# Four graph-attention layers on one core: fewer factor columns from one transfer, a front in halves with the activation table first, and a last output closed head by head

## The chip, the cores and the metric

The kernel runs on one core of one Trainium2 chip. The metric is the device time in microseconds. Before the change it is 3103.57 us, the median of three runs (3102.70 to 3105.31); the profiled execution took 3104.86 us and its profile spans 3103.1 us. The program holds two versions of the computation: a fast one, and a slow general one that is entered only if a flag says that the inputs leave the fast one's assumptions. In these runs only the fast one works.

Names used below: PE is the matrix engine (TensorE), DVE the vector engine, ACT the scalar engine with its activation tables, POOL is GpSimd, SP the engine that issues most transfers.

## What is computed

The input `x` is 16 batches of 1024 nodes with 256 features, `adj` is one 1024 x 1024 integer adjacency matrix. Four layers follow each other, each of them `x = x + layer(relu(layernorm(x)))`:

```python
# --- layer 0 (adj_preln) ---
h = jnp.maximum(_layernorm(x, axis=-1), 0.0)
x = x + _L0_gnn_ref(h, adj, L0_gnn_W, L0_gnn_a)
# layers 1, 2 and 3 in the same way, with _L1_, _L2_ and _L3_

# layer 0 (4 heads of 64 features; layers 1 and 3 differ in heads and mask only)
Wh = (h @ W).reshape(h.shape[0], h.shape[1], N_H, D_F)
a_src, a_dst = (a[:, :D_F], a[:, D_F:])
s_src = jnp.einsum('bnhd,hd->bnh', Wh, a_src)
s_dst = jnp.einsum('bnhd,hd->bnh', Wh, a_dst)
e = s_src[:, :, None, :] + s_dst[:, None, :, :]
e = jnp.where(e > 0, e, NEG_SLOPE * e)          # NEG_SLOPE = 0.2
e = jnp.where(mask, e, -jnp.inf)
alpha = jax.nn.softmax(e, axis=2)
h_out = jnp.einsum('bijh,bjhd->bihd', alpha, Wh)
return jax.nn.elu(h_out)
```

Layers 0 and 3 have four heads of 64 features, layer 1 has one head of 256. Layer 2 scores by a product of two projections of the nodes (512-wide products) instead of by two columns, and ends in a relu.

In layers 0, 1 and 3 the kernel needs no exponential for each pair of nodes. With `s_i` for the source and `s_j` for the other node, `exp(leaky(s_i + s_j))` is, up to a factor that only depends on `i` and falls out of the softmax, `exp(s_j) * max(exp(0.8 s_i), exp(-0.8 s_j))`. So three exponentials for each node and head are enough: `exp(s_j)` scales the values, `exp(0.8 s_i)` is spread as a row (`row`), and `exp(-0.8 s_j)` is a column (`ke`). The exponents come out of the projection itself: the weights `w` carry a few more columns, the products of `W` and `a`.

## The kernel before

A small scheduler (`Plan`) collects every step with its engine, an assumed cost and a due time, and lays all batches and layers into one order for each engine. The due times follow from constants:

```python
PERIOD, EARLY = 190.0, 0.39
START = {0: 0.0, 1: 0.9852, 2: 2.2118, 3: 3.5247}
LEAD = {0: 0.62, 1: 0.38, 2: 0.32, 3: 0.87}
STEP = {0: 0.0465, 1: 0.0464, 2: 0.0538, 3: 0.0718}
# WHEN, LATER and AHEAD: shifts for single layers and batches (left out)
```

Each engine runs its own list strictly in that order, so a step that waits holds up everything behind it on its engine.

The weights and their factor columns, three for each head. `first` is the weight of layer 0, whose columns DVE makes; for the others POOL multiplies and ACT adds up:

```python
t = const.tile([P, KC, F + 3 * heads], F32, name=name)
...
def load_a():
    tiles["a"] = buf("p1", [P, 2, heads, d], name="a_bc")
    for side in range(2):
        queue.dma_start(
            out=tiles["a"][:, side],
            in_=bass.AP(tensor=a.tensor, offset=a.offset + side * side_step,
                        ap=[[0, P], [head_step, heads], [1, d]]),
        )
...
for c in range(KC):
    for side, to in ((1, 0), (0, 2)):
        # columns: wa = W[c] * a[side]              (DVE or POOL, L666)
        # add_up:  sum over d into column(s), with
        scales = (1.0, SLOPE - 1.0) if side else (1.0 - SLOPE,)
```

The prologue of a layer: statistics of `x`, then the reciprocal deviation (DVE L833, POOL L836, DVE L839), the normed rows `h` on ACT (L870), their transposes on PE (L886), a copy to SBUF on ACT (L901), the projection on PE, and the eviction:

```python
cols = F + 3 * heads if self.gat else F
...
product(pv[:, :cols], T["hT", t0][:, c, k * P : (k + 1) * P], w[:, c, :cols], ...)
...
a = self.val[:, t, :, d : d + 1]
nc.scalar.activation(a, T["pv", t][:, F : F + heads].unsqueeze(2), AF.Exp)               # L931
nc.scalar.activation(self.ke[:, :, t], T["pv", t][:, F + heads : cols], AF.Exp)          # L932
```

`product` splits each stationary tile into two of 64 columns, and the profile shows two matmuls for each of these in float32. The first layer of the first batch has its statistics in one piece, ahead of the first `rstd`:

```python
due, step = SOON, 0.1
stats = [statistics(b, t, due - 1, (loads[b][t],)) for t in range(NT)]
```

The attention of the layers with four heads. `weigh` runs on DVE, `attend` on PE; each `p` tile of 128 x 512 feeds four products, which are 16 matmuls of 65 columns in the profile:

```python
nc.vector.scalar_tensor_tensor(          # L1063
    p, lay.rows[half, hd], lay.ke[:, hd, jt : jt + 1], mask_of(half, jt), op0=OP.max, op1=OP.mult)
...
product(T["acc", half, hd][:, t, :], p[:, t * P : (t + 1) * P], lay.val[:, jt, hd, :], ...)
```

When a head is summed, it is divided by its denominator; after the last head of a half of the nodes the elu, the residual and, in layer 3, the store are done for all heads together:

```python
if hd != heads - 1:
    continue
its = (half * HT, (half + 1) * HT)
s = lay.elu(T, half, its, at - early[0], (s,), (4, 2.3, 2.45), ("o",))
# elu: ACT exp (L1035), ACT relu(1 - exp) (L1036), DVE max (L1040), DVE add to x (L1041)
```

Of the kernel before, what the change touches and what calls it, by code (L numbers as in the profile page):

```python
# [44 lines left out]
PERIOD, EARLY = 190.0, 0.39  # L45
START = {0: 0.0, 1: 0.9852, 2: 2.2118, 3: 3.5247}
LEAD = {0: 0.62, 1: 0.38, 2: 0.32, 3: 0.87}
STEP = {0: 0.0465, 1: 0.0464, 2: 0.0538, 3: 0.0718}
WHEN = {
    (1, "weights"): ((-0.3018, 0.0087), (-0.0444, 0.0088)),  # L50
    (1, "attended"): ((0.2222, 0.0273), (0.109, 0.1164)),
    (2, "weights"): ((0.0221, 0.0304), (0.2823, 0.0096)),
    (2, "attended"): ((0.438, 0.0374), (0.6199, 0.0376)),
# [3 lines left out]
    (0, 3): 0.058, (1, 0): 0.06, (1, 1): 0.618, (2, 0): -0.057, (2, 1): -0.091, (3, 0): -0.332, (3, 1): -0.137,  # L57
    (3, 2): 0.022, (12, 2): 0.228, (12, 3): 0.316, (13, 1): 0.259, (13, 3): 0.414, (14, 1): -0.085,
    (14, 2): 0.134, (14, 3): -0.14, (15, 1): -0.188, (15, 2): 0.165, (15, 3): -0.487,
}  # L60
AHEAD = {
    (0, 3): -0.158, (1, 0): 0.374, (2, 0): 0.124, (2, 1): -0.123, (3, 2): -0.288, (15, 2): -0.045,
    (15, 3): -0.78,
# [7 lines left out]

# [460 lines left out]
def fast(  # L532
# [95 lines left out]
    def weight(w, name, due, a=None, heads=0, side_step=0, head_step=0):  # L628


        t = const.tile([P, KC, F + 3 * heads], F32, name=name)

        def load():
            queue.dma_start(out=t[:, :, :F], in_=w.rearrange("(c p) f -> p c f", p=P))

        queue = nc.scalar if name == "w0" else nc.sync
        engine = ACT if name == "w0" else SP
        s = landed(plan.add(engine, 0.5, due, load), due, 256)
        if a is None:
            return t, s  # L640
        d = F // heads
        tiles = {}

        def load_a():
            tiles["a"] = buf("p1", [P, 2, heads, d], name="a_bc")
            for side in range(2):
                queue.dma_start(
                    out=tiles["a"][:, side],
                    in_=bass.AP(
                        tensor=a.tensor,  # L650
                        offset=a.offset + side * side_step,
                        ap=[[0, P], [head_step, heads], [1, d]],
                    ),
                )

        s2 = landed(plan.add(engine, 1.2, due, load_a, take=("p1",)), due, 256)


        first = name == "w0"
        done = []  # L660
        for c in range(KC):
            for side, to in ((1, 0), (0, 2)):

                def columns(c=c, side=side, to=to):
                    wa = tiles["wa", c, side] = buf("u", [P, heads, d], name="wa")
                    (nc.vector if first else nc.gpsimd).tensor_mul(  # L666
                        wa, t[:, c, :F].rearrange("p (h d) -> p h d", h=heads), tiles["a"][:, side]
                    )

                def add_up(c=c, side=side, to=to):  # L670
                    wa, lo = tiles.pop(("wa", c, side)), F + to * heads
                    scales = (1.0, SLOPE - 1.0) if side else (1.0 - SLOPE,)
                    if first:
                        nc.vector.tensor_reduce(t[:, c, lo : lo + heads], wa, AX.X, OP.add)
                    for k, scale in reversed(list(enumerate(scales))):
                        to_all = t[:, c, lo + k * heads : lo + (k + 1) * heads]
                        if first:
                            if scale != 1.0:
                                nc.vector.tensor_scalar(to_all, t[:, c, lo : lo + heads], scale, None, op0=OP.mult)
                            continue  # L680
                        for hd in range(heads):
                            junk = small.tile([P, F], BF16, name="junk_a", bufs=1)[:, :d]
                            nc.scalar.activation(  # L683
                                junk, wa[:, hd, :], AF.Identity, scale=scale, accum_out=to_all[:, hd : hd + 1]
                            )

                last = c == KC - 1 and side == 0
                give = ("u", "p1") if last else ("u",)
                after = (s, s2, *done[-1:])
                m = plan.add(*((DVE, 0.4) if first else (POOL, 1.0)), due + 0.5, columns, after, take=("u",))  # L690
                cost = 0.65 if first else (1 + side) * (1.0 if heads > 1 else 0.4)
                done.append(plan.add(DVE if first else ACT, cost, due + 0.5, add_up, (m,), give=give))
        return t, done[-1]

    first_x = load_x(0, SOON)
    w0, w0_ready = weight(w_l0, "w0", SOON, a_l0, 4, F // 4, F // 2)
# [38 lines left out]
    w1, w1_ready = weight(w_l1, "w1", 20.0, a_l1, 1, F, 2 * F)  # L735
    w2v, w2v_ready = weight(w3_l2, "w2v", 30.0)
    w3, w3_ready = weight(w_l3, "w3", 50.0, a_l3, 4, F // 4, 0)
# [68 lines left out]
    class Layer:  # L806
# [7 lines left out]
        def prologue(self, due, step, stats, direct=False):  # L814
# [6 lines left out]
            cols = F + 3 * heads if self.gat else F  # L821
# [5 lines left out]
            for n, its in enumerate(parts):  # L827
# [26 lines left out]
                s = plan.add(DVE, 0.2, due, norm, (*stats[its], ready[-1] if n else None))  # L854
                s = plan.add(POOL, 2.0, due, norm2, (s,))
                take = () if n else (tag,) if self.gat else (tag, "hq")
                ready += [plan.add(DVE, 0.2, due, norm3, (s,), take=take)] * (its.stop - its.start)
# [35 lines left out]
            for n, t0 in enumerate(range(0, NT, 2)):  # L893
# [11 lines left out]
                for k in range(2):  # L905
# [18 lines left out]
                    def evict(t=t):  # L924
# [6 lines left out]
                        nc.scalar.activation(a, T["pv", t][:, F : F + heads].unsqueeze(2), AF.Exp)  # L931
                        nc.scalar.activation(self.ke[:, :, t], T["pv", t][:, F + heads : cols], AF.Exp)  # L932
# [41 lines left out]
            if direct:  # L974
                for half in range(2):
                    for hd in range(heads):

                        def spread(half=half, hd=hd):
                            pd = T["pd", half, hd] = buf("pp", [P, HALF])
                            for k in range(HT):  # L980
                                col = self.ke[:, heads + hd, half * HT + k : half * HT + k + 1]
# [14 lines left out]
            def factors():  # L996
                er = T["er"] = buf("pp", [P, P])
                nc.tensor.transpose(er[:n, :], self.ke[:, heads:, :].rearrange("p h t -> p (h t)"), ident)  # L998
# [29 lines left out]
        def elu(self, T, key, its, due, after, sizes, give):  # L1028

            tag = f"ex{sizes[0]}"  # L1030
            xs = lambda: x_tiles[self.b][:, its[0] : its[1], :]

            def up():
                T["ex", key] = buf(tag, [P, its[1] - its[0], F])
                nc.scalar.activation(T["ex", key], T["o", key], AF.Exp)  # L1035
                nc.scalar.activation(T["ex", key], T["ex", key], AF.Relu, bias=1.0, scale=-1.0)  # L1036

            def down():
                o, ex = T["o", key], T["ex", key]
# [3 lines left out]
            s = plan.add(ACT, sizes[1], due, up, after, take=(tag,))  # L1043
            s = plan.add(DVE, sizes[2], due, down, (s,), give=(tag, *give))
            for t in range(its[0], its[1]):
                self.finish(t, due, (s,))
# [5 lines left out]
    def steps_a(lay, due, span):  # L1052
# [4 lines left out]
        for i in range(n):  # L1057
# [56 lines left out]
            if hd != heads - 1:  # L1114
                continue
# [289 lines left out]
```

## Time and profile before, and how to read them

| what | value |
|---|---|
| median of three runs | 3103.57 us |
| span of the profile | 3103.1 us |
| PE busy | 3058.2 us |
| DVE busy | 2716.4 us |
| ACT busy | 1354.5 us |
| POOL busy | 128.3 us |
| DMA over the span | 123.22 MB, mean 40 GB/s |

The page of the profile first gives the busy time of each engine, then the busy share in 40 equal slices of the span (77.6 us each), the DMA queues, the chain of work that ended last, and the groups of instructions by line, with their count, busy time and mean length. A matmul's end is modelled and matmuls overlap in the pipeline, so the mean length of a single one is much longer than the distance from one to the next, and a PE that is shown busy need not be at its best rate. Besides the page, the trace answers for parts of the span: a timeline of instructions (start, length, engine, line, what is written and read, and in brackets the idle time before and what ended it), the busy time of each engine in windows, the chain of waits in order of time, and the same groups kept apart by shape.

### The profile page before, as it was taken

The numbers are of one execution on the slowest core, as the hardware profiler recorded it, in microseconds if no ns is written. First come the engines' busy times: TensorE is split into PE (matmuls) and PEld (weight loads), VectorE is DVE, ScalarE is ACT, GpSimd is POOL, SyncE is SP. The second block draws the span as 40 slices with busy tenths as digits, with TensorE's granted clock in tenths as the row PEclk, the third lists the DMA queues.
The fourth block names the chain that finished last, engine by engine and source line by source line (L and its number), as shares of the span: only waits on it lengthen the run. The fifth ranks groups of instructions, "written<-read, shape, count | busy, mean of one in ns | idle before, by whom it ended". The sixth has DMA issues, their size and how long they took to land.

```text
span 3103.1 us, 108725 instructions
## 1 busy us (share of the span) xinstructions
PE 3058.2 (99%) x48836; PEld 2160.0 (70%) x48836; DVE 2716.4 (88%) x5532; ACT 1354.5 (44%) x3369; POOL 128.3 (4%) x99
## 2 busy tenths in 40 slices
PE   7899999999999999999999999999999999999998
PEld 5776757777676776767767676676767767665766
DVE  7999868999989899898989989899899989787797
ACT  5454465443533445334443433434334453345343
POOL 1000000000000000000000000000000000000000
PEclk9999999999999999999999999999999999999999
DMA  3111002102011110101102011020111101000110
GB/s 127 33 54 33 19 29 73 46 30 60 22 40 46 36 46 23 60 23 36 46 26 60 23 36 47 26 60 22 43 43 33 53 30 39 19 22 29 33 36 24
DMA packets 83577, 123.22 MB, mean 40 GB/s; under 512 B 8544, under 2 KB 44192, under 8 KB 83104
## 3 DMA queue, kind: packets, MB, share of 16 engines
q1 hardware_dynamic: 81776, 115.66, 12.4%
q8 instruction: 385, 6.31, 0.8%
q14 instruction: 88, 0.72, 0.1%
q10 hardware_dynamic: 1328, 0.52, 0.1%
HBM read 98.83 MB, written 17.33 MB: 37 GB/s over the span
## 4 chain that ended last, share of the span: by engine, by line
PE 96%; DVE 2%; DMA 1%; ACT 0%; issue 0%; POOL 0%; SPq 0%; POOLq 0%; DVEq 0%
PE pp L574 32%; PE acc L574 31%; PE accb L574 29%; PE pp L886 4%; DVE p L1063 1%; DMA a_bc<-in_L_gnn_a_dram 1%; DMA raw<-in_adj_dram 0%; DVE bn L800 0%; PE pp L998 0%; DVE xt L1041 0%; PE pp L982 0%; DVE o L1040 0%; DVE mv L801 0%; ACT junk_a L683 0%; POOL rstd L836 0%
## 5 line engine op out<-in xcount | busy, mean ns | idle before, releaser
L1063 DVE SCALAR_TENSOR_TENSOR p<-row,ke,mask 128x512 f32<-128x512 f32 x2048 | 1424.5, 745 | 94.5 <-PE acc L574 91.7
L574 PEld LDWEIGHTS acc<-val,p 128*64 128x64 f32 x32768 | 1066.9, 138 | 202.0 <-issue 109.0
L574 PE MATMUL acc<-val,p 128*64 128x65 f32 x32768 | 1095.4, 223 | 12.1 <-DVE p L1063 11.1
L574 PE MATMUL accb<-val,p 128*64 128x257 f32 x8192 | 926.1, 380 | 0.0
L574 PEld LDWEIGHTS accb<-val,p 128*64 128x64 f32 x8192 | 569.7, 136 | 291.3 <-issue 9.5
L574 PE MATMUL pp<-qT,hT 128*64 128x512 f32 x2048 | 471.5, 593 | 0.0
L574 PE MATMUL pp<-w,hTp 128*64 128x268 f32 (+1 forms) x3072 | 376.3, 388 | 0.7 <-ACT hTp L901 0.7
L1169 ACT ACTIVATE u<-pp 128x512 f32<-128x512 f32 x256 | 152.4, 595 | 323.2 <-PE pp L574 229.4
L574 PEld LDWEIGHTS pp<-w,hTp 128*64 128x64 f32 x3072 | 209.6, 137 | 107.8 <-issue 6.2
L870 ACT ACTIVATE h<-xt,nshift,rstd 128x256 f32<-128x256 f32 x512 | 272.5, 595 | 17.0 <-DVE nshift L839 15.7
L574 PEld LDWEIGHTS pp<-qT,hT 128*64 128x64 f32 x2048 | 133.0, 137 | 190.4 <-issue 184.9
L1209 ACT ACTIVATE o<-accb,rdens 128x256 f32<-128x256 f32 x128 | 60.7, 474 | 424.8 <-DVE rdens L1201 384.9
L800 DVE BATCH_NORM_STATS2 bn<-xt 128x6 f32<-128x256 f32 x512 | 212.5, 415 | 13.6 <-DMA xt<-in_x_dram 4.3
L836 POOL TENSOR_TENSOR rstd<-rstd,neg_half 128x8 f32<-128x8 f32 (+1 forms) x66 | 119.6, 1813 | 2371.9 <-DVE rstd L833 2094.5
L1207 ACT ACTIVATE o<-accb,rden 128x256 f32<-128x256 f32 x128 | 60.7, 475 | 336.4 <-DVE rden L1201 335.5
L1175 DVE TENSOR_TENSOR p<-p,mask 128x512 f32<-128x512 f32 x256 | 177.1, 692 | 8.9
L1142 DVE SCALAR_TENSOR_TENSOR p<-row,ke,mask 128x512 f32<-128x512 f32 x256 | 181.1, 743 | 0.0
L1174 DVE SCALAR_TENSOR_TENSOR p<-u,p 128x512 f32<-128x512 f32 x256 | 174.5, 682 | 5.9 <-ACT p L1170 5.7
L1170 ACT ACTIVATE p<-pp,shift_col 128x512 f32<-128x512 f32 x256 | 174.9, 683 | 0.0
L931 ACT ACTIVATE val<-pp 128x4 f32<-128x4 f32 (+1 forms) x384 | 66.8, 174 | 202.3 <-PE pp L574 202.2
L1040 DVE SCALAR_TENSOR_TENSOR o<-ex,o 128x256 f32<-128x256 f32 (+1 forms) x192 | 131.8, 686 | 16.0 <-ACT ex L1036 16.0
L901 ACT COPY hTp<-pp 128x512 f32<-128x512 f32 x192 | 104.6, 588 | 88.7 <-PE pp L886 88.6
(82 smaller groups left out, 1849.8 us busy)
## 6 DMA issues: line engine op xcount, KB each, us to landing
row<-er_d SPq DMA_DIRECT2D x272, 256.0 KB, 3.2
xt<-in_x_dram SPq DMA_DIRECT2D x32, 512.0 KB, 5.1
out_dram<-xt SPq DMA_DIRECT2D x32, 512.0 KB, 3.1
raw<-in_adj_dram SPq DMA_DIRECT2D x4, 1024.0 KB
raw<-in_adj_dram SPq DMA_DIRECT2D x16, 256.0 KB, 3.2
w<-in_L_gnn_W_dram SPq DMA_DIRECT2D x2, 256.0 KB
a_bc<-in_L_gnn_a_dram SPq DMA_DIRECT2D x4, 128.0 KB, 10.3
wraw<-in_L_gnn_W_dram SPq DMA_DIRECT2D x2, 256.0 KB
```

The lines of the kernel that those rows point to most:

```text
L574: nc.tensor.matmul(to[c : c + COLS], stationary[:, c : c + COLS], moving, start=start, stop=stop, skip_group_check=True,)
L800: nc.vector.bn_stats(st, x_tiles[b][:, t, :])
L836: nc.gpsimd.tensor_tensor(T["rstd"][:, its], T["rstd"][:, its], neg_half[:, its], OP.pow)
L870: nc.scalar.activation(h, x_tiles[b][:, t, :], AF.Relu, bias=T["shift"][:, t : t + 1], scale=T["rstd"][:, t : t + 1],)
L886: nc.tensor.transpose(tp[:, c, k * P : (k + 1) * P], T["h", t0 + k][:, c * P : (c + 1) * P], ident)
L1040: nc.vector.scalar_tensor_tensor(o, ex, -1.0, o, op0=OP.mult, op1=OP.max)
L1063: nc.vector.scalar_tensor_tensor(p, lay.rows[half, hd], lay.ke[:, hd, jt : jt + 1], mask_of(half, jt), op0=OP.max, op1=OP.mult)
L1142: nc.vector.scalar_tensor_tensor(p, lay.rows[half, 0], lay.ke[:, 0, jt : jt + 1], mask_of(half, jt), op0=OP.max, op1=OP.mult)
L1169: nc.scalar.activation(u, e, AF.Exp, scale=1.0 - SLOPE)
L1170: nc.scalar.activation(p, e, AF.Exp, bias=shift_col, scale=SLOPE)
L1174: nc.vector.scalar_tensor_tensor(p, u, 1.0, p, op0=OP.max, op1=OP.mult)
L1175: nc.vector.tensor_mul(p, p, mask_of(half, jt))
```

## The change

The change has five parts.

1. **A factor column less for each head.** `exp(s_j)` is no longer read from a column of its own. The column `-0.8 s_j` is there already, and the activation's scale of `1 / (SLOPE - 1)` turns it back. The projection of layers 0 and 3 has 264 columns in place of 268, that of layer 1 has 258 in place of 259.
2. **`a` from one transfer.** Both sides of `a` come in one contiguous piece for each partition; the factors 0.8 and -0.8 are put on `a` itself by two DVE operations (L656 after the change) instead of on the sums. For layer 3, whose `a` is shared by the heads, only one copy is loaded.
3. **The front.** Statistics and `rstd` of the first half of the nodes are placed ahead of those of the second half, and a dummy exponential on ACT loads the activation table ahead of the first needed activation.
4. **The end.** In the last half of the last layer of the last batch, elu and residual are done head by head, the division of the last head moves from ACT to DVE, and the store is split into the first three heads and the last.
5. **New constants** for the scheduler, which change the order of the work on every engine.

```diff
-PERIOD, EARLY = 190.0, 0.39
-START = {0: 0.0, 1: 0.9852, 2: 2.2118, 3: 3.5247}
+PERIOD, EARLY = 190.0, 0.56
+START = {0: 0.0, 1: 0.9446, 2: 2.175, 3: 3.5153}
 ... (LEAD, STEP, WHEN, LATER and AHEAD in the same way)
-        t = const.tile([P, KC, F + 3 * heads], F32, name=name)
+        t = const.tile([P, KC, F + 2 * heads], F32, name=name)
 ...
-            for side in range(2):
-                queue.dma_start(
-                    out=tiles["a"][:, side],
-                    in_=bass.AP(... ap=[[0, P], [head_step, heads], [1, d]]),
+            queue.dma_start(
+                out=tiles["a"].rearrange("p h s d -> p (h s d)"),
+                in_=bass.AP(tensor=a.tensor, offset=a.offset, ap=[[0, P], [1, own * 2 * d]]),
+            )
+        def sign():
+            for side, by in enumerate((1.0 - SLOPE, SLOPE - 1.0)):
+                of = tiles["a"][:, :, side, :]
+                nc.vector.tensor_scalar(of, of, by, None, op0=OP.mult)
 ...
+    def warm():
+        nc.scalar.activation(faults[:, 0:1], ones, AF.Exp)
+    plan.add(ACT, 1.6, SOON, warm)
 ...
-            cols = F + 3 * heads if self.gat else F
+            cols = F + 2 * heads if self.gat else F
 ...
+                at = due - 2 * (direct and n == 0)
+                s = plan.add(DVE, 0.2, at, norm, (*stats[its], ready[-1] if n else None))
 ...
-            nc.scalar.activation(a, T["pv", t][:, F : F + heads].unsqueeze(2), AF.Exp)
-            nc.scalar.activation(self.ke[:, :, t], T["pv", t][:, F + heads : cols], AF.Exp)
+            nc.scalar.activation(
+                a, T["pv", t][:, F + heads : cols].unsqueeze(2), AF.Exp, scale=1.0 / (SLOPE - 1.0))
+            nc.scalar.activation(self.ke[:, :, t], T["pv", t][:, F:cols], AF.Exp)
 ...
+            ending = lay.b == B - 1 and lay.layer == 3 and half == 1
+            on_act = lay.filling and not (ending and hd == heads - 1)
 ...
-            if hd != heads - 1:
+            if ending:
+                cols, sizes = (hd * d, (hd + 1) * d), (4, 0.8, 0.8)
+            elif hd == heads - 1:
+                cols, sizes = (0, F), (4, 2.3, 2.45)
+            else:
                 continue
 ... (elu on these columns; the store after head 2 takes three heads, that after head 3 the last)
-            stats = [statistics(b, t, due - 1, (loads[b][t],)) for t in range(NT)]
+            stats = [statistics(b, t, due - (3 if t < HT else 1), (loads[b][t],)) for t in range(NT)]
```

## The prediction

> **What bounds the kernel now.** First the page: engine totals and slices.
>
> ```profile
> PE 3058.2 (99%) x48836; PEld 2160.0 (70%) x48836; DVE 2716.4 (88%) x5532; ACT 1354.5 (44%) x3369; POOL 128.3 (4%) x99
> ...
> PE   7899999999999999999999999999999999999998
> ```
>
> PE is busy nearly always; only the first and the last slices (77.6 us each) fall short. But a busy PE may still be stretched, so I ask at what distance matmuls follow each other at best. The chain of waits, in order of time, gives runs of one kind:
>
> ```profile
> 1136.62 6.07 PE acc L574 x208
> 1158.21 10.44 PE accb L574 x96
> 1198.04 6.87 PE pp L574 x32
> 1220.15 3.61 PE pp L574 x32
> 1346.52 10.44 PE accb L574 x96
> ```
>
> So 29.2 ns for 65 columns (6.07/208), 108.75 ns for 257, 214.7 ns for 512 and 113 ns for 268; a 128-wide transpose takes 127.5 ns (8 in 1.02 us, same view). The run of 96 `accb` comes back after 188.31 us: that is the steady state, one batch.
>
> Counts by shape (the groups kept apart by shape) times these distances: 32768 x 29.2 = 957 us, 8192 x 108.75 = 891, 2560 of 512 columns 550, 2048 of 268 columns 232, 1024 of 259 and 1024 of 256 about 223 (interpolated), 1142 transposes 146, masks and the rest 7. **Sum: 3004 us.** The span is 99 us above this floor. I place those 99 by counting the PE instructions that stand, in the built order, before two moments of the trace:
>
> - The first `accb` run starts at 142.3 us; 94.7 us of PE work stand before it. Lost: 47.6 us, the **front**.
> - PE's product for the final check is at 3041.1 us; 39.5 us of work follow within 62.0 us. Lost: 22.5 us, the **tail**.
> - Between them: 2898.8 us for 2870 us of work. Lost: 29 us, 1%, spread evenly; changes between 128-wide and 64-wide stationary tiles (364 in the whole order) fit it, at some 0.08 us each.
>
> The front's PE timeline and DVE timeline:
>
> ```profile
> 83.23 18.78 PE L574 MATMUL acc<-val,p 128*64 128x65 f32 x448 [2.57 <-DVE p L1063]
> 107.00 6.10 PE L574 MATMUL acc<-val,p 128*64 128x65 f32 x112 [4.99 <-DVE p L1063]
> ```
>
> 448 matmuls in 18.78 us are 41.9 ns each, not 29.2: PE counts as busy, but DVE sets the pace (0.67 us for each `p`, which feeds 16 matmuls or 0.47 us of PE). So in the front PE's loss is DVE's lateness. DVE's idle gaps there:
>
> ```profile
> 13.08 0.42 DVE L666 TENSOR_TENSOR wa<-w,a_bc 128x256 f32<-128x256 f32 x1 [2.82 <-DMA a_bc<-in_L_gnn_a_dram]
> ...
> 17.06 0.16 DVE L839 SCALAR_TENSOR_TENSOR nshift<-mv,rstd 128x4 f32<-128x4 f32 x1
> ...
> 29.24 2.74 DVE L1063 SCALAR_TENSOR_TENSOR p<-row,ke,mask 128x512 f32<-128x512 f32 x4 [0.30 <-ACT row L986]
> ...
> 38.10 0.76 DVE L940 TENSOR_TENSOR val<-pp,val 128x256 f32<-128x256 f32 x2 [2.67 <-ACT ke L932]
> ```
>
> DVE stands still for `a`; `nshift`, ready since 11.4 us, is computed at 17.06 because it stands behind `a` and the masks, and ACT loads its table only after it (17.29, 1.28 us). The second stop is ACT's: it sits behind the column sums of layer 3's weight, POOL behind their `a`:
>
> ```profile
> 34.15 1.88 POOL L666 TENSOR_TENSOR wa<-w,a_bc 128x256 f32<-128x256 f32 x2 [11.62 <-DMA a_bc<-in_L_gnn_a_dram]
> ```
>
> The tail's timeline:
>
> ```profile
> 3092.53 0.18 DVE L1096 RECIPROCAL rden<-acc 128x4 f32<-128x4 f32 x1 [0.79 <-PE acc L574]
> 3092.75 0.93 ACT L1107 ACTIVATE o<-acc,rden 128x64 f32<-128x64 f32 x4 [3.99 <-DVE rden L1096]
> 3093.71 1.06 ACT L1035 ACTIVATE ex<-o 128x1024 f32<-128x1024 f32 x1
> 3094.79 1.06 ACT L1036 ACTIVATE ex<-ex 128x1024 f32<-128x1024 f32 x1
> 3095.88 1.23 DVE L1040 SCALAR_TENSOR_TENSOR o<-ex,o 128x1024 f32<-128x1024 f32 x1 [3.17 <-ACT ex L1036]
> 3097.14 1.23 DVE L1041 TENSOR_TENSOR xt<-xt,o 128x1024 f32<-128x1024 f32 x1
> ```
>
> Nothing overlaps here: 5.84 us from the last reciprocal to the last add, then 4.7 us until the span ends (the store).
>
> **What the skill says.** The Trainium skill, "TensorE: Matmul & The Clock Gate", section "Wait — 56ns, not 53.3ns?", puts matmuls at N / 2.4 GHz plus about 2.5 ns when warm; the trace is within 2 ns (113 for 268, against 114), so a column less is worth what the width says. "Perfetto Trace Analysis", "Identifying the Most-Contended Engine", warns that PE's busy share misleads; the 41.9 ns above are such a case. "ScalarE: Activation LUTs", "What ACT_TABLE_LOAD costs", gives about 1283 ns for the load; the trace has 1.28 us. "DMA: Bandwidth & Descriptors", "Specifications", asks for 512 bytes or more in a piece; the old `a_bc` has 256-byte pieces where there are four heads, and its transfers land 8.3 to 10.3 us after issue, agreeing in direction.
>
> **The change, part by part.**
>
> *Columns.* From 268 to 512 columns the distance grows by 101.7 ns in 244, 0.416 ns a column. 2048 matmuls lose four columns (3.4 us) and 1024 lose one (0.4 us): **-3.8 us** on the bound engine, nearly all of it in the saturated middle, so it reaches the end.
>
> *Front.* Before the first `p`, DVE's new order is: four statistics, `rstd`, four statistics (to about 10.3 us, as now), two sign operations, `nshift`, two multiplications (about 12.2), then masks, the second two multiplications and the second sum. I add it up with today's lengths (0.42 for a mask step or a multiplication, about 0.7 for a 512-element sum), allow 0.5 us for the first mask quarter, and have `w0` ready at 18.7 us. Then PE has six projections (6 x 0.9), four transposes and the first row's spread, ACT its copy: first `p` near 25.9 us instead of 29.24, **-3.3**. The transposes and `h`, freed by the earlier `nshift` and the table, are ready long before; `w0` is what ends last. After the first `p` the remaining DVE work is nearly equal (four mask copies more, three fewer already done, two `val` fewer: +0.4 us net), but the 2.67 us stop and about 1 us of smaller ones beside it should go, if layer 3's `a` (64 KB in 512-byte pieces instead of 256 KB in 256-byte pieces) lands early: **-3**. Later in the front the new order puts the 512-wide products of layer 2 among the `p`s sooner, where PE waited for DVE between 177 and 198 us (about 3.4 us lost): perhaps **-1**. Together **-7 us**.
>
> *Middle.* 358 instead of 364 changes of width: -0.5 us. The new constants can neither win much (29 us of switching stay) nor are they meant to lose.
>
> *Tail.* The last `accb` now stands with the first half's transposes behind it, and all four of its projections follow; from the last `accb` to the first `p` I count 3.6 us of projections, 0.5 spread, 0.6 copy and an eviction, about 5.5 us against 7.8 now: -2.3. Then DVE is the bound again (64 `p`s in 47.1 us now, with no idle time worth a line), and three elu slices move into its list: 3 x 0.75 = +2.3, plus perhaps 1 us of waiting for ACT. After the last `p`: reciprocal, division on DVE (0.42), two ACT operations of 256 elements (about 0.5 each), two DVE operations (0.42 each), 2.4 us with hand-overs instead of 5.84: -3.4. The store shrinks from 512 to 128 KB: -0.5. Sum **-3 us**.
>
> Total: 3.8 + 7 + 0.5 + 3 = 14.3 us; 3103.6 - 14.3 = **3089.3 us**, a factor of 0.9954.
>
> **Rivals.**
>
> 1. *The sign operations take the place of the removed wait.* They stand on DVE, in order, and those of layers 1 and 3 stand ahead of the first `p`. Layer 3's `a` landed at 34.0 us. For it: DVE cannot pass a late transfer. Against it: the new transfer has 128 pieces instead of 1024, and the DMA slices from 22 us on were not full. If it lands after 30 us the front gains nothing: about 3096 us.
> 2. *The front is DVE-bound anyway, the start is hidden.* An earlier start only helps if the later DVE list is gapless. For it: nearly no gap from 40 to 113 us. But a gapless list shifts as a whole, so the start does count; what does not count is PE's own waiting. Time: 3090 to 3094 us if new gaps appear further on.
> 3. *The new order is the larger effect.* If it holds a bubble somewhere in the saturated middle, or DVE falls behind late (two stretches near the end of the order ask DVE for 19 to 21 us of `p` in 25 us of PE work, where before it was 17 to 19): 3095 to 3105 us. If it fills the front or shortens the steady period: 3078 to 3083 us.
> 4. *The tail's slices cancel.* Work moved onto the bound engine eats what the end saves: about 3092 us.
>
> **Range and chances.** The columns are sure to within 0.5 us, front and tail each to about 4 us, the order to about 5. Eight in ten: 3080 to 3098 us. For 2% the kernel would have to fall under 3041.5 us, 62 of the 99 us above the floor and nearly all of front and tail together: 0.01. Slower by 2%: 0.01. Within 2%: 0.98.
>
> **What would show it.** Right: 264-column runs of 32 near 3.56 us; the steady period near 188.0 us; first `p` at 25 to 27 us; no 2.67 us DVE wait for ACT near 38 us; no table load behind `nshift`; under 3 us from the last reciprocal to the last add; about 40 us lost before the first `accb` run and about 20 after the final check. Wrong: a DVE wait for `a_bc` above 2 us ahead of the first `p`; PE idle time between 200 and 3000 us; a tail of over 62 us.

## The result, and the profile after

The changed kernel takes **3088.34 us** (median of 4 runs, 3087.85 to 3089.07), the kernel before in the same session 3103.51 (3102.7 to 3105.31). The ratio is 0.9951 with a 95% interval of 0.9933 to 0.9968: 15.2 us gained. The profiled spans are 3086.9 and 3103.1 us; places in time below are of these profiles. A span is 1.8 us shorter than the time of its own execution. The profiled execution of before (3104.86 us) was 1.4 us above its median, that of after (3088.70 us) 0.4 us, so 1.0 of the 16.2 us between the spans is no gain. Gains are therefore compared median with median, and the trace is used to place them.

The page of after, engine totals and 40 slices:

```profile
PE 3048.6 (99%) x48836; PEld 2170.7 (70%) x48836; DVE 2720.0 (88%) x5551; ACT 1350.4 (44%) x3352; POOL 130.5 (4%) x99
...
PE   7999999999999999999999999999999999999998
```

Little of the result is to be seen here: PE's busy time fell by 9.6 us, and the second slice went from 8 to 9, since the front ends earlier. The chain of waits in the middle, first a run of 32 matmuls of 264 columns, then one that comes back with each batch:

```profile
928.79 3.56 PE pp L573 x32
...
1012.15 4.54 PE pp L573 x32
...
1200.23 4.54 PE pp L573 x32
```

With 264 columns such a run takes 3.56 us, with 268 it took 3.61. The last run comes back after 188.08 us; one batch took 188.31. The difference of 0.23 us a batch is what the narrower products are worth: with 111.4 ns for 264 columns in place of 113, and so on for layer 1, the floor of the prediction (the sum of counts times distances) falls by 3.9 us to 3000.4. That is the first part. The other 12.3 of the 16.2 us of span are time that PE lost before and loses no more.

DVE's timeline of after, the front (start, length, engine, line, operation, count, and in brackets the idle time before):

```profile
11.65 0.16 DVE L843 SCALAR_TENSOR_TENSOR nshift<-mv,rstd 128x4 f32<-128x4 f32 x1
...
25.03 0.28 DVE L656 TENSOR_SCALAR a_bc<-a_bc 128x64 f32<-128x64 f32 x2
25.27 1.29 DVE L1075 SCALAR_TENSOR_TENSOR p<-row,ke,mask 128x512 f32<-128x512 f32 x1
...
30.45 0.74 DVE L948 TENSOR_TENSOR val<-pp,val 128x256 f32<-128x256 f32 x2
```

`nshift` of the first half stands at 11.65 us instead of 17.06, the first `p` at 25.27 instead of 29.24. None of these lines has a bracket: the stop of 2.67 us, which stood ahead of two `val` operations near 38 us, is gone (they are at 30.45), and DVE does not wait for layer 3's `a` either (its sign operations at 25.03). PE's timeline of the same stretch:

```profile
76.23 19.18 PE L573 MATMUL acc<-val,p 128*64 128x65 f32 x448 [2.60 <-DVE p L1075]
100.40 4.79 PE L573 MATMUL acc<-val,p 128*64 128x65 f32 x112 [4.99 <-DVE p L1075]
...
134.74 10.61 PE L573 MATMUL accb<-val,p 128*64 128x257 f32 x96
```

448 matmuls in 19.18 us are 42.8 ns each, as slow as before: DVE still sets the pace here. The stretch was not made faster, it begins earlier. The first `accb` run starts at 134.74 instead of 142.1 us.

Lost time is what is left of a stretch after the counts of its matmuls times their distances are taken off:

| us | before | after |
|---|---|---|
| 0 to 50 | 27.3 | 21.8 |
| 50 to 100 | 9.8 | 14.3 |
| 100 to 150 | 9.8 | 3.1 |
| 150 to 200 | 3.9 | 0.0 |
| 0 to 200 | 50.8 | 39.2 |

So 11.6 us came from the first 200 us. (Between 50 and 100 us after loses more, because the stretch that DVE paces, with its stop of 4.99 us, now lies there; in before that stop fell behind 100 us.) In the tail the loss after the final check's product is 22.2 us (it was 22.5), in all the rest it is 0.4 less than before. With the 3.9 us of columns these make the 16.2. DVE's timeline of the end:

```profile
3029.94 2.74 DVE L1075 SCALAR_TENSOR_TENSOR p<-row,ke,mask 128x512 f32<-128x512 f32 x4 [2.50 <-ACT row L994]
...
3079.87 0.18 DVE L1108 RECIPROCAL rden<-acc 128x4 f32<-128x4 f32 x1 [0.79 <-PE acc L573]
3080.09 0.42 DVE L1119 TENSOR_TENSOR o<-acc,rden 128x256 f32<-128x256 f32 x1
3081.44 0.42 DVE L1051 SCALAR_TENSOR_TENSOR o<-ex,o 128x256 f32<-128x256 f32 x1 [0.93 <-ACT ex L1047]
3081.90 0.42 DVE L1052 TENSOR_TENSOR xt<-xt,o 128x256 f32<-128x256 f32 x1
```

From the last reciprocal to the end of the last add are 2.45 us instead of 5.84. But from the end of the last `accb` run to the first `p` it is 7.6 us, as before (7.6), with 2.50 us of waiting for ACT's copy of the row. ACT's timeline shows what stands ahead of that copy:

```profile
3026.88 2.08 ACT L875 ACTIVATE h<-xt,nshift,rstd 128x256 f32<-128x256 f32 x4 [0.69 <-DVE nshift L843]
3028.86 0.56 ACT L906 COPY hTp<-pp 128x512 f32<-128x512 f32 x1
3029.33 1.06 ACT L994 COPY row<-pp 128x512 f32<-128x512 f32 x2
```

### The profile page after: what moved, and what is told of

It is laid out like the page before. It is cut to its first block, busy times and chain, and to the rows that moved or that the text cites. A ratio compares the mean times of both kernels' runs of the same rounds, so it can differ in the third digit from the quotient of the medians.

```text
span 3086.9 us, 108696 instructions
## 1 busy us (share of the span) xinstructions
PE 3048.6 (99%) x48836; PEld 2170.7 (70%) x48836; DVE 2720.0 (88%) x5551; ACT 1350.4 (44%) x3352; POOL 130.5 (4%) x99
## 3 DMA queue, kind: packets, MB, share of 16 engines
q1 hardware_dynamic: 81248, 115.47, 12.3%
## 4 chain that ended last, share of the span: by engine, by line
PE 96%; DVE 4%; issue 0%; DMA 0%; ACT 0%; SPq 0%; ACTq 0%; DVEq 0%
PE pp L573 32%; PE acc L573 30%; PE accb L573 29%; PE pp L891 4%; DVE p L1075 2%; DVE bn L804 0%; PE pp L1006 0%; DMA xt<-in_x_dram 0%; DVE xt L1052 0%; DVE mv L805 0%; DVE o L1051 0%; DVE val L948 0%; DVE pos L719 0%; PE tpm L726 0%; PE pp L990 0%
## 5 line engine op out<-in xcount | busy, mean ns | idle before, releaser
L573 PEld LDWEIGHTS accb<-val,p 128*64 128x64 f32 x8192 | 581.4, 136 | 275.2 <-issue 9.8
L573 PE MATMUL pp<-w,hTp 128*64 128x264 f32 (+1 forms) x3072 | 363.8, 385 | 0.0
L891 PE MATMUL pp<-ident,h 128*128 128x128 f32 x1024 | 141.6, 281 | 1.0 <-ACT hTp L906 1.0
L1052 DVE TENSOR_TENSOR xt<-xt,o 128x256 f32<-128x256 f32 (+1 forms) x195 | 133.3, 684 | 6.7
```

What stands on the lines that cost most here:

```text
L573: nc.tensor.matmul(to[c : c + COLS], stationary[:, c : c + COLS], moving, start=start, stop=stop, skip_group_check=True,)
L891: nc.tensor.transpose(tp[:, c, k * P : (k + 1) * P], T["h", t0 + k][:, c * P : (c + 1) * P], ident)
L1052: nc.vector.tensor_add(xs(), xs(), o)
```

## The experiments

The variants "after without one part" are to be compared with 3088.34 us, the variants "before with one part" with 3103.0 to 3103.5, which is what the kernel before took in each session. After was timed in one session alone; that before moved by no more than 0.5 us from session to session is the ground for comparing across them. Kernels with the same front start their first `accb` run between 134.7 and 135.7 us, so differences below 1 us are not read as effects.

**1. The columns back.** The removed columns return as zeros; places and order stay those of after.

```diff
-        t = const.tile([P, KC, F + 2 * heads], F32, name=name)
+        t = const.tile([P, KC, F + 3 * heads], F32, name=name)
+        if heads:
+            nc.gpsimd.memset(t[:, :, F + 2 * heads :], 0.0)
...
-            cols = F + 2 * heads if self.gat else F
+            cols = F + 3 * heads if self.gat else F
```

> The changed kernel with the removed columns put back as zero columns: 268 and 259 columns are projected, the order on every engine and everything else stay. Theory (PE bounds the middle and a column costs what its width says): 2048 x 4 x 0.416 ns + 1024 x 0.416 ns = 3.8 us more, 3092.1 us, with 268-column runs of 32 back at 3.61 us from 3.56. Rival (the middle has slack, what counts is front and tail): within 0.5 us of 3088.3.

Measured: 3092.45 us (ratio to before 0.9965, 0.9953 to 0.9978), 4.1 above after. In the trace the runs of 32 are back at 3.61 us and a batch at 188.32. The columns are worth what their width says.

**2. The old transfer of `a`.** Pieces of 256 bytes, and four copies for layer 3's heads.

```diff
-            queue.dma_start(out=tiles["a"].rearrange("p h s d -> p (h s d)"), in_=... [[0, P], [1, own * 2 * d]])
+            for side in range(2):
+                queue.dma_start(out=tiles["a"][:, :, side, :],
+                    in_=... [[0, P], [2 * d if own == heads else 0, heads], [1, d]])
```

> The changed kernel with a loaded as before, two transfers and 256-byte pieces where there are four heads, four copies for layer 3; steps and order stay. Theory (the transfer is what held DVE and ACT in the front, and the sign operations would now be held by it): layer 3's a lands near 30 to 34 us instead of before 25, the first p comes 5 to 9 us later than 25.3 us, the end 5 to 9 us later, 3093 to 3097 us. Rival (the transfers are hidden behind the masks' 4 MB in any case): within 1.5 us of 3088.3.

Measured: 3097.09 us (0.9981, 0.9974 to 0.9989), 8.7 above after. DVE's timeline:

```profile
13.03 0.29 DVE L660 TENSOR_SCALAR a_bc<-a_bc 128x256 f32<-128x256 f32 x1 [2.26 <-DMA a_bc<-in_L_gnn_a_dram]
...
32.93 0.29 DVE L660 TENSOR_SCALAR a_bc<-a_bc 128x256 f32<-128x256 f32 x1 [5.58 <-DMA a_bc<-in_L_gnn_a_dram]
33.14 0.74 DVE L1079 SCALAR_TENSOR_TENSOR p<-row,ke,mask 128x512 f32<-128x512 f32 x1
```

The sign operation of layer 3 waits 5.58 us for its late `a`, and the first `p` stands behind it. This is rival 1 of the prediction: a true danger, and the new transfer is what kept it away. The transfers of the first 60 us, first in after, then here:

```profile
DMA packets 7351, 9.60 MB, mean 160 GB/s; under 512 B 304, under 2 KB 5040, under 8 KB 7344
...
DMA packets 9318, 9.78 MB, mean 163 GB/s; under 512 B 2400, under 2 KB 7264, under 8 KB 9312
```

There are 304 packets under 512 bytes in after and 2400 here. Besides the size of the pieces, the number of transfers and, for layer 3, the bytes differ (four copies instead of one); which of the three counts was not tried apart.

**3. The one transfer alone, in the kernel before.** Its order, columns, statistics and end are kept.

> The kernel before with only its transfer of the attention vector as one contiguous piece per layer (one head's vector once for all heads in layer 3); the order, the columns, the statistics and the end are those of before. Theory A (the late transfer is the largest part of the front's gain, as the opposite run showed with 8.7 us): DVE's wait for it of 2.82 us and the stop near 38 us of 2.67 us are gone or small, first p 2 to 3 us earlier than 29.24, time 4 to 8 us below before: 3095.5 to 3099.5 us. Theory B (the table load behind nshift and the whole statistics then end last): first p less than 1.5 us earlier, time 1 to 3 us below before.

Measured: 3100.69 us (0.9993, 0.9984 to 1.0002), 2.3 below before, and the interval reaches 1. Three lines of DVE's timeline:

```profile
11.36 0.42 DVE L662 TENSOR_TENSOR wa<-w,a_bc 128x256 f32<-128x256 f32 x1
...
15.33 0.16 DVE L836 SCALAR_TENSOR_TENSOR nshift<-mv,rstd 128x4 f32<-128x4 f32 x1
...
27.66 2.74 DVE L1060 SCALAR_TENSOR_TENSOR p<-row,ke,mask 128x512 f32<-128x512 f32 x4 [0.30 <-ACT row L983]
```

The wait of 2.82 us is gone (no bracket at 11.36), but `nshift` still stands behind the masks, and the first `p` comes 1.6 us earlier only. The first `accb` run starts 4.6 us earlier (table below); the time shows half of that, and the high execution of before in the trace is part of the difference. The same part is worth 8.7 us in one direction and 2.3 in the other. One reason stands in the traces: in after the sign operations make DVE itself wait for layer 3's `a` if it is late (5.58 us in run 2), while in before that transfer held POOL (11.62 us) and, behind it, ACT. How much the other parts add to the difference is not shown.

**4. No halves.** The statistics of the first layer in one group again.

```diff
-                at = due - 2 * (direct and n == 0)
+                at = due
...
-            stats = [statistics(b, t, due - (3 if t < HT else 1), (loads[b][t],)) for t in range(NT)]
+            stats = [statistics(b, t, due - 1, (loads[b][t],)) for t in range(NT)]
```

> The kernel after with the statistics of the first batch's first layer in one piece: the second half's statistics and the whole normalisation stand ahead of nshift again, all else as after. Theory A (h is early anyway, w0's columns end last ahead of the first p): first p at 25.0 to 25.8 us against 25.27, projections still near 17.9 us, time 0 to 0.7 us above after, that is 3088.3 to 3089.1 us. Theory B (the halves carry part of the earlier start): nshift near 13 to 14 us instead of 11.65, first p 1 us or more later, 3089.3 to 3090.5 us.

Measured: 3093.20 us (0.9969, 0.9957 to 0.998), 4.9 above after: theory A falls, and the loss is larger than B's as well. DVE's timeline:

```profile
15.78 0.15 DVE L843 SCALAR_TENSOR_TENSOR nshift<-mv,rstd 128x4 f32<-128x4 f32 x1
...
27.49 0.43 DVE L719 TENSOR_SCALAR pos<-raw 128x512 bf16<-128x512 int32 x1 [1.29 <-PE pp L891]
...
29.21 2.73 DVE L1075 SCALAR_TENSOR_TENSOR p<-row,ke,mask 128x512 f32<-128x512 f32 x4
```

The columns of `w0` are done at 17.6 us in both kernels. Yet the first projection starts at 19.63 instead of 17.93, since `h` can only follow `nshift`; so in this kernel `w0` is not what ends last. Most of the loss comes later: between 25 us and the first `accb` run DVE stands still 8.8 us instead of 3.4, mostly waiting for PE, whose first accumulations are late. What was undone is the halving together with the place in the queue that its due times give it; the two were not tried apart. The first of the two edits also reaches the last layer of the last batch; from the last `accb` run to the end it is 64.4 us here and 64.6 in after, so the loss is not there.

**5. No dummy exponential.**

> The changed kernel without the dummy exponential, the order otherwise kept: the table load of 1.28 us comes ahead of the first h, from about 11.7 us. Theory of the prediction (the weight's factor columns end last, h and transposes are ready long before): 0 to 0.3 us more. Rival (PE is held in its list by the transposes of h, behind it stand masks, whose copies stand in DVE's list ahead of the second column sum): the first p comes 1.0 to 1.3 us later and so does the end, 3089.5 us.

Measured: 3088.92 us (0.9954, 0.9938 to 0.9971), no effect that can be told from 0. ACT's timeline shows why:

```profile
6.04 1.28 ACT L875 ACT_TABLE_LOAD   x1 [6.04 <-DMA xt<-in_x_dram]
```

The load stands ahead of the first `h`, and its bracket names the transfer of `x` and not DVE: the 1.28 us pass at 6 us, long before `nshift` at 11.7. In before it stood at 17.29, behind `nshift`, and its bracket names DVE. Something else in the change had thus already moved it, and the dummy exponential adds nothing. The transfer or the order alone did not do it (runs 3 and 7 have the load at 15.56 and 17.51 us, behind `nshift`).

The traces point to the halves. Ahead of the first `h` ACT has an instruction that only waits for semaphores (the signals between engines). The view of `h`'s line lists these (count; shortest, median and longest in ns; first and last start in us), in run 4 and in after:

```profile
L875 ACTq EVENT_SEMAPHORE  x103: 17/17/10261, 5.7 to 2736.6; - x103
...
L875 ACTq EVENT_SEMAPHORE  x105: 17/17/1616, 5.8 to 2732.3; - x105
```

In run 4 the first of them, at 5.7 us, is the long one: ACT's list stands for 10.26 us, until `nshift` is there, and `h` starts at 16.02. In after the first one is over in 0.02 us, and so it is in runs 1, 2, 6 and 12. A load with the waits that ACT has in run 4 would stand behind `nshift` as in before. No run leaves out the halves and the dummy exponential together, so this is not shown directly.

**6. and 7. The order.** Once after with the old constants, once before with the new ones.

> The kernel after with the constants of the order of before: columns, transfer, halves and closing head by head stay. Theory A (the trace of after: the order is worth what was lost between 150 and 200 us, 3.4 us, and half a microsecond of width changes in the middle): 3 to 5 us above after, 3091.3 to 3093.3 us. Theory B (the order only matters in what the prediction gave it, 1 us in the front and 0.5 in the middle): 3089.3 to 3090.5 us. Theory C (the constants were found for the new costs and the old ones fit badly): over 3095 us.

> The kernel before with only the constants of the new order. Theory A (the order is worth 3 to 5 us on its own, whatever the front does): 3098.5 to 3100.5 us. Theory B (the order pays only when DVE is no longer late from the stop near 38 us): 3102 to 3104 us, no difference. Theory C (it is worse with the old front): over 3105 us.

Measured: after with the old order 3093.04 us (0.9969, 0.9957 to 0.998), 4.7 above after; before with the new order 3098.99 us (0.9988, 0.9981 to 0.9995), 4.0 below before. Where the order acts shows in the loss between 150 and 200 us: 3.9 us in before, 4.1 in the two variants with the old order (runs 3 and 6), and 0.2 or less in every variant with the new one. PE's groups between 150 and 200 us in after show what fills it:

```profile
L573 PE MATMUL pp<-hT,w 128*64 128x512 f32 x32 | 7.0, 592 | 0.0
L573 PE MATMUL pp<-qT,hT 128*64 128x512 f32 x10 | 2.3, 592 | 0.0
```

These are 42 products of layer 2 with 512 columns, 9.3 us of PE's time that read no `p`; in before there is none of them in that stretch. The order is worth 4 to 5 us with either front, most of it there.

**8. The last half closed as a whole.** `ending = False`.

> The changed kernel with the last half closed for all four heads at once, as before; the order up to there stays. Theory: after the last p 3.6 us longer (11.4 instead of 7.8), the DVE list ahead of it 2.0 us shorter (47.1 instead of 49.1): 1.6 us more, 3090 us. Rival (slices on the bound engine cancel or cost): 3088 us or less.

Measured: 3089.83 us (0.9957, 0.994 to 0.9973), 1.5 above after; from the last `accb` run to the end 66.2 us instead of 64.6. Before took 66.1 us, so the closing head by head is all that the tail gained.

**9. The row copies sooner at the end.** In the tail ACT copies the first row ahead of the second half's four `h`; this goes after the wait of 2.50 us.

```diff
+ # in the last layer of the last batch, after the row copy of (half 0, head 0) is added:
+ for k in late:                      # the steps of the second half's h
+     plan.steps[k][4] += (self.row_ready[half, hd],)
```

> The kernel after, where in the last layer of the last batch ACT copies the first row of factors ahead of the second half's four normalisations, so that the first p need not stand behind them. Theory A (the four h, 2.08 us, and a copy of transposes hold the first p, 2.50 us of DVE waiting for ACT): first p about 2 us sooner after the last accb run (5.5 to 6 us instead of 7.8), end 1.5 to 2.2 us sooner, 3086.1 to 3086.9 us. Theory B (the second half's projections then come late and DVE waits further on): first p sooner, but the last p not, 3087.8 to 3088.8 us.

Measured: 3088.74 us (0.9954, 0.9937 to 0.997), no gain. DVE's timeline:

```profile
3028.00 2.74 DVE L1079 SCALAR_TENSOR_TENSOR p<-row,ke,mask 128x512 f32<-128x512 f32 x4 [0.23 <-ACT row L995]
3033.12 0.42 DVE L949 TENSOR_TENSOR val<-pp,val 128x256 f32<-128x256 f32 x1 [2.38 <-ACT ke L941]
```

The first `p` does come 2 us sooner, and after four of them DVE waits 2.38 us for the second half's `ke`, which the later `h` delay. The wait has changed its place.

**10. and 11. A part of the `p` on POOL.** If DVE's 0.67 us for each `p` is the bound at the ends, an idle POOL could take one of eight, in two operations and into a buffer of its own: once in the last layer, once in the first as well.

```diff
+            other = (lay.b, lay.layer) == (B - 1, 3) and jt == HT     # run 11: also (0, 0)
...
+                if other:
+                    nc.gpsimd.tensor_scalar(p, lay.rows[half, hd], of, None, op0=OP.max)
+                    nc.gpsimd.tensor_tensor(p, p, mask_of(half, jt), OP.mult)
+                    return
```

> The kernel after, where in the last layer of the last batch one p of each row of eight is computed by POOL (two operations, maximum and product with the mask), ahead of its turn and into a buffer of its own. Theory A (DVE's 0.67 us for each p is what sets the tail): DVE has 8 x 0.67 = 5.4 us less to do, first to last p 49.1 -> about 44 us, time 4 to 5.5 us below after: 3082.8 to 3084.3 us. Theory B (POOL is too slow for one p in 4.7 us, or slows DVE beside it): PE or DVE waits for POOL, or DVE's p takes more than 0.67 us, and the gain is under 2 us.

> As the run before, in the first layer of the first batch as well. Theory A (the front is DVE's pace too): first accb run a further 3 to 5 us sooner, and since the middle is full, the same in the time: 3078 to 3081.5 us. Theory B (POOL stands behind the products for layer 3's columns until about 36 us, so its first p come late and PE waits): no gain over the run before, or a loss. Theory C (the front's second half, where 512-wide products and layer 1's p come, is not bound by these p): a gain of 1 to 2 us.

Measured: 3092.84 us (0.9969, 0.9956 to 0.9981) and 3097.07 us (0.9981, 0.9973 to 0.9989): 4.5 and 8.7 slower than after. POOL's timeline and DVE's beside it, in the first of the two:

```profile
3042.12 1.99 POOL L1080 TENSOR_SCALAR p<-row,ke 128x512 f32<-128x512 f32 x1
3044.19 1.26 POOL L1081 TENSOR_TENSOR p<-p,mask 128x512 f32<-128x512 f32 x1
...
3041.13 6.63 DVE L1083 SCALAR_TENSOR_TENSOR p<-row,ke,mask 128x512 f32<-128x512 f32 x6
...
3076.51 2.73 DVE L1083 SCALAR_TENSOR_TENSOR p<-row,ke,mask 128x512 f32<-128x512 f32 x4
```

While POOL works, six `p` of DVE take 6.63 us, 1.10 each; when it is done, four take 2.73, 0.68 each. A `p` on POOL lasts 3.3 us; DVE makes three in that time where it had made five. One `p` is won and two are lost. Taken one by one, the `p` are not slowed evenly. This one starts while POOL's product of 3044.19 us runs:

```profile
3044.36 1.64 DVE L1083 SCALAR_TENSOR_TENSOR p<-row,ke,mask 128x512 f32<-128x512 f32 x1
```

It takes 1.64 us, where a `p` without POOL is recorded with 0.74, and ends 0.55 us after POOL's product (3045.45). The same 0.55 us lie between the end of POOL's product and the end of the `p` beside it for all eight products of this run: the `p` stands until the product is through. A `p` that starts during POOL's first operation takes at most 1.18 us. The Trainium skill, "SBUF — State Buffer", section "Who interferes with whom", says that a DVE instruction with two inputs in SBUF contends with a GpSimd instruction that reads SBUF, and calls the ports that the two share "an exclusive lock". The 0.55 us agree with this.

**12. DVE's waits at both ends.** Tail: run 9, and the `p` of the second head's first half ahead of those of the first head's second half, so that DVE has eight to do during the wait. Front: the first row is spread ahead of the other half's projections, to bring the first `p` forward.

```diff
+        turns = [(i // (heads * NT), i // NT % heads, i % NT) for i in range(n)]
+        if (lay.b, lay.layer) == (B - 1, 3):
+            turns[: 2 * NT] = sorted(turns[: 2 * NT], key=lambda q: (q[2] >= HT, q[1], q[2]))
...
+                        if (b, half, hd) == (0, 0, 0):
+                            for k in projections[HT:]:
+                                plan.steps[k][4] += (s,)          # s: the spread of the first row
```

> The kernel after with an edit at each end, aimed at DVE's waits. Front: in the first layer of the first batch the first row of factors is spread as soon as the first half's factors are there, ahead of the other half's projections. Tail: the row copy ahead of the second half's normalisations as in the earlier run, and the p of the second head's first half ahead of the p of the first head's second half, so that DVE has eight p to do, not four, until the second half's values come. Theory A (DVE is the bound at both ends, and time that it stands still is time lost): front, first p at about 23.3 instead of 25.27 us and first accb run 1.5 to 2 us sooner; tail, no 2.38 us wait, from the last accb run to the end 2 us less than 64.7; together 3084 to 3085.5 us. Theory B (PE or ACT hold the second half up by as much in the front; the middle absorbs it): the front gives nothing, 3086 to 3087 us. Theory C (neither end gains): 3088 to 3089 us.

Measured: **3086.33 us** (5 runs, 3085.56 to 3087.21; ratio to before 0.9945, 0.9931 to 0.9958), 2.0 below after; the two ranges of times do not overlap, the intervals of the ratios do. The two ends are told apart in the trace. DVE's timeline, first the front and then the tail:

```profile
24.04 0.75 DVE L1088 SCALAR_TENSOR_TENSOR p<-row,ke,mask 128x512 f32<-128x512 f32 x1
...
3027.76 5.39 DVE L1088 SCALAR_TENSOR_TENSOR p<-row,ke,mask 128x512 f32<-128x512 f32 x8 [0.23 <-ACT row L998]
3033.07 0.41 DVE L951 TENSOR_TENSOR val<-pp,val 128x256 f32<-128x256 f32 x1
```

In the tail neither wait is left, and the stretch from the last `accb` run to the end is 62.9 us instead of 64.6. In the front the first `p` is 1.2 us earlier, and the first `accb` run starts at 134.85 us instead of 134.74: no gain that could be read.

**One sum that places the fronts.** I added up all idle times that DVE's timeline shows ahead of the first `accb` run:

| kernel | first `p` | DVE idle to 25 us | from there on | sum | first `accb` run |
|---|---|---|---|---|---|
| before | 29.24 | 11.8 | 9.7 | 21.5 | 142.11 |
| before, new order (7) | 30.10 | 10.6 | 7.8 | 18.4 | 140.73 |
| before, one transfer (3) | 27.66 | 10.7 | 6.3 | 17.1 | 137.50 |
| after, old transfer (2) | 33.14 | 11.4 | 11.0 | 22.4 | 143.60 |
| after, no halves (4) | 29.21 | 9.0 | 8.8 | 17.8 | 139.28 |
| after, columns back (1) | 26.07 | 10.6 | 3.8 | 14.4 | 136.06 |
| after, old order (6) | 25.44 | 10.0 | 3.9 | 14.0 | 134.48 |
| after | 25.27 | 9.9 | 3.4 | 13.2 | 134.74 |
| both ends (12) | 24.04 | 9.8 | 3.2 | 13.1 | 134.85 |
| after, POOL at both ends (11) | 24.86 | 9.5 | 5.5 | 15.0 | 138.67 |

In the first nine rows the last two columns move together: from before to after 8.3 us less of standing still and 7.4 us earlier, without the halves 4.6 more and 4.5 later, with the old transfer 9.2 more and 8.9 later. The first `p` does not tell it: kernels 4 and before have it at the same time and differ by 2.8 us, and kernel 12 has it first and wins nothing. Runs 5, 8, 9 and 10 share after's front: sums of 13.7 to 14.2, starts of 135.3 to 135.7 us. About 5.5 us of each sum is the wait for the first piece of `x`.

The sum is bookkeeping: idle and busy time of one engine always add up to the moment at which one stops counting. What the table shows is that DVE's work up to there hardly changes. The start less the sum is 120.5 to 120.6 us in the three kernels with the old order and 121.2 to 122.3 in the six with the new one, where two more `p` stand ahead of it (for the new order in before, 3.1 us less of idling and only 1.4 earlier). So what the parts change is how long DVE stands still. Where its work itself gets longer, the sum alone misleads: with POOL at both ends it is 1.7 us more than in after, but the `accb` run starts 3.9 us later, although DVE has eight `p` fewer to make.

## Why the prediction was right, and where its steps were not

The time was predicted as 3089.3 us and is 3088.34; the gain is 15.2 us where 14.3 were expected. In the spans of the traces the four terms (columns, front, middle, tail) are 3.9, 11.6, 0.4 and 0.3 us, together 16.2; the prediction has 3.8, 7, 0.5 and 3. So the mechanism was found, and the sum is as close as it is partly by luck: the front's terms were too small by 4.6 us, the tail's too large by 2.7, and the executions that were profiled differ by 1.0 us more than the medians.

- **Columns, -3.8: right.** The period fell by 0.23 us a batch, the floor by 3.9; taken back, they cost 4.1.
- **Front up to the first `accb` run, -6: the mechanism right, the size -8.2** (lost 47.6, now 39.4, as "about 40" foresaw, though by a sum that gave only 6). The first `p` at 25.27 (predicted near 25.9) and the vanished stop are as predicted. The start of the `accb` run moved by 7.4 us, from 142.1 (the prediction reads 142.3 from the chain of waits), and somewhat more PE work now stands ahead of it. The mis-sized term is "about 1 us of smaller ones": apart from the 2.67, the stops after 25 us fell from 7.0 to 3.4, by 3.6 us. The estimate was made with the first `p` and a single stop; the sum of DVE's standing times was the right measure.
- **`h` and its transposes "are ready long before; `w0` is what ends last": the first half is wrong.** In after the transposes ahead of the first projection end only as it begins, at 17.93 us, and `w0` is done at 17.6 (predicted 18.7). The two end within 0.3 us of each other, and the trace puts the last 0.33 us of waiting down to `w0`:

```profile
17.93 5.09 PEld L573 LDWEIGHTS pp<-w,hTp 128*64 128x64 f32 x48 [0.33 <-DVE w L679]
```

Run 4 shows that without the halves `h` is last by 2 us. That `h` would be ready "long before" did not allow for its transposes standing behind mask transposes on PE.

- **The table load: right that it leaves `nshift`'s shadow**, but the dummy exponential was not needed for it (run 5); the traces point to the halves instead.
- **"Perhaps -1" for the order later in the front: too small, -3.9** (runs 6 and 7). The place was right, between 150 and 200 us, and so was the means, layer 2's products of 512 columns; the loss there is gone as a whole.
- **Middle, -0.5: not contradicted.** The trace gives 0.4, which is less than can be read from it.
- **Tail, -3: only about half, -1.5,** counted as in the prediction from the last `accb` run (66.1 us, now 64.6). Of this, some 0.6 us is PE work that now stands ahead of that run or has become narrower; lost time after the final check fell by 0.3 us alone, to 22.2 where "about 20" was expected. The step that failed is -2.3 for the first `p` (from 7.8 us as the prediction reads it, 7.6 by DVE's timeline, to 5.5; it stayed 7.6): it counted PE's work and one copy, and overlooked that ACT has four `h` (2.08 us) and a copy of transposes ahead of the row. Run 9 shows that even when it comes in time it is worth nothing by itself, run 12 that it needs other `p` to fill the time until the second half's values. The slices on DVE cost 2.0 (predicted 2.3), the end after the last `p` gave 3.5 (11.3 us, now 7.9; predicted 3.9 with the store).

Of the rivals, the first was shown to be real and avoided (run 2), the second did not occur (only 3.4 us of new and old stops are left between 25 us and the first `accb` run), the third holds in part: the order is worth 4.7 us, as much as the halves, and in the place that the rival gave it, by filling the front. The fourth holds in part too: the slices took back 2.0 of the 3.5 us that the end saved. The parts do not add up: taken away one at a time they cost 4.1, 8.7, 4.9, 0.6, 4.7 and 1.5 us, together 24.5 against 15.2. Several act on the same list of DVE, where taking one away uncovers a wait that the others had made harmless. The transfer is the clearest case (8.7 us in after, 2.3 in before), while the order is worth about the same in both (4.7 and 4.0). What stays open is the share of the halves apart from their place in the queue, which property of the new transfer counts, and a direct test of what moved the table load.

## What to carry to other kernels

Where an engine works through a fixed list and sets the pace, add up all its idle times up to the end of that stretch. As long as its work there stays the same, that sum, and not when its first important instruction starts, tells what an earlier transfer or a moved step is worth. Before moving work to an idle engine, see whether the busy one gets slower beside it (here from 0.68 to 1.10 us for each `p`). And price a part both by taking it away from the new version and by adding it alone to the old: the transfer was worth 8.7 us in one and 2.3 in the other.

## What I had not expected of the hardware

- POOL beside DVE: DVE operations on tiles of 128x512 went from 0.68 to 1.10 us each, averaged over six, while POOL ran its two operations (1.99 and 1.26 us) on tiles of the same size. A single `p` took up to 1.65 us and ended 0.55 us after POOL's product, eight times out of eight.
- The way a small vector is loaded can hold more than the step that needs it: with the old transfers of `a` (2400 packets under 512 bytes instead of 304 in the first 60 us) DVE's wait for layer 3's `a` was 5.58 us instead of none, and the first `p` came 7.9 us later.
- The table load can pass before all inputs of its activation are there: 1.28 us at 6.04 us, for an `h` that ran at 11.92. In before it stood at 17.29, and its bracket names DVE instead of the transfer.
